# One more slot in seven-product form, and a longer searched order, in a gated MLP kernel

## The chip, the cores and the metric

The kernel runs on one core of a Trainium2 chip. The metric is device time in microseconds (us) of one execution. The core's engines are TensorE (PE; its weight loads are listed as PEld), VectorE (DVE), ScalarE (ACT), GpSimd (POOL) and the sync engine (SP), which issues most DMA transfers. Each engine runs its own row of instructions in order and waits for the others at semaphores.

## What is computed

For each of 4 batches, with 1024 tokens of 512 values:

```
scale = cond @ norm_w.T + 1.0
ms = jnp.mean(x * x, axis=-1, keepdims=True)
h = x * (scale[:, None, :] * jax.lax.rsqrt(ms + EPS))
u = h @ up_w.T                       # up_w: 4096 x 512
val, gate = jnp.split(u, 2, axis=-1)
h = val * jax.nn.gelu(gate, approximate=False)
y = act_quant(h) @ weight_quant(down_w).T
return y + x
```

`act_quant` rounds each token to 8 bits by its largest value, `weight_quant` makes the weights ternary.

## The kernel before

**Work.** The up-projection goes in 16 slots per batch; slot j holds 128 columns of the value and 128 of the gate, for 1024 tokens in two halves. x^T and the weights are split into high and low fp16 parts, and three of the four partial products are summed. A slot comes in one of two forms. The *plain* form (`plain_half`, `plain`, matmul line L1156) takes 12 matmuls of 128x512 for each of value and gate and each half of the tokens, 48 in all. The *seven-product* form (`slot`, `product`, matmul line L1141) treats a slot as 2x2 blocks and makes seven block products of 6 matmuls, 42 in all; it needs sums of weight blocks and sums of x blocks, and more additions behind the matmuls (ACT copies at L1219, L1227 and L1231, gelu at L1236 and L1252; DVE at L1239, L1249, L1255 and L1258, where the plain form has L1180 on ACT and L1184 on DVE). Which slots of the first batch are plain is set by one constant, `SEVEN = 9` (L808): slots 0 to 8 plain, 9 to 15 in seven products. The later batches have seven products throughout. The down-projection (L1362, L1413) is interleaved from the second batch on.

**Weights.** They are loaded once (L774, L777), scaled by a power of two found from their largest value (range L786, L659, L793, L796; scaling L815 on ACT, L817 on POOL), turned (on PE for the first slots, L825 with the copies L850, L852, L853 and L859 to L862; by turning DMA for later ones, L840 to L842), summed (L867 to L870), split (L880, L884) and spilled to DRAM (L888; from slot 9 on, turned first, L895). The later batches load them back: sum parts of slots below `SEVEN` by turning DMA (L909), the others as they are (L911).

**The start.** A condition row is spread over the partitions by a matmul (L685), multiplied with `norm_w` on DVE (L690), shifted (L706), its largest value found (L708, matmul L715, L721), made a power of two (L659, L725), spread again (L731) and inverted (L735, L738). Beside it the sums of squares of the four first blocks of x are taken (L1480 on ACT, L1482 on DVE), POOL makes the reciprocal root (L1001, L1002), the blocks are scaled (L1487 on ACT, L1489 on DVE and POOL), turned on PE (L1494) and split (L1498 on ACT, L1502 on DVE). The first half slot (`plain_first`, L1199) uses them. Warm-up matmuls whose results nobody uses (`keep_warm`, L1510) stand between: 3, 5, 2 and 13 of them.

**Order.** The code does not run in the order in which it is written. Every operation is recorded as a step, with its dependences and an estimated price. `order` places the steps by due time, then goes through a list of seeds: for each one `mend` replays the rows of the engines with randomly changed durations, takes a wait of PE and shifts due times in the chain that led to it. At the end `moved` takes the list `MOVES`: each pair takes one step out of its engine's row and puts it ahead of another. A warm-up matmul has the same price in this model as any other 128x512 matmul.

Of the kernel before, what the change touches and what calls it, by code (L numbers as in the profile page):

```python
# [115 lines left out]
class Plan:  # L116
# [71 lines left out]

    def order(self):

        steps = self.steps
        for s in steps:
            s.after, s.cost, s.soon, s.queue = [], s.alone, 0.0, None
        for s in steps:
            s.pre = [(steps[d], lag(steps[d], s)) for d in s.deps]
            for d in s.deps:
                steps[d].after.append(s)
        clock = 0.0
        self.matmuls = [s for s in steps if s.eng == "PE"]
        for s in self.matmuls:  # L200
            s.start = clock
            clock += s.cost
        chance = random.Random(1)
        self.lucks = [[(chance.random(), chance.random()) for _ in steps] for _ in range(MISSES)]
        for n in range(ROUNDS):
            margin, guard, chained, crowded = MARGINS[n % len(MARGINS)]
            self.needed(clock, chained)
            if crowded:
                self.crowd()
            for s in steps:  # L210
                s.margin, s.guard = margin, guard
            order, kept = self.placed()
            clock = self.replay(order)
        for n in MENDS:
            order, kept = self.mend(order, kept, random.Random(n))
        return self.moved(order)

    def moved(self, order):
# [12 lines left out]
        self.replay([s for row in rows.values() for s in row])  # L231
        return sorted(self.steps, key=lambda s: (s.start, s.n))

    def placed(self):

        kept = [(s.late, s.margin, s.guard, s.soon, s.cost) for s in self.steps]
        self.place()
        return sorted(self.steps, key=lambda s: (s.start, s.n)), kept

    def mend(self, order, kept, chance):  # L240

        steps, last, waits = self.steps, 0.0, []
        for s, k in zip(steps, kept):
            s.late, s.margin, s.guard, s.soon, s.cost = k
        clock = self.replay(order, chance.choice(self.lucks))
        for s in order:
            if s.eng == "PE":
                if s.start - last > 0.08:
                    waits.append((s.start - last, s))
                last = s.end  # L250
        s = chance.choices([s for _, s in waits], [w for w, _ in waits])[0]
        chain, swap, q = [], None, s.behind
        while q is not None and q.eng != "PE" and len(chain) < 20:
            chain.append(q)
            p = q.queue or q.behind
            if p is not None and p.n not in q.deps and chance.random() < 0.5:
                swap = chance.random() < 0.6 and p.eng != "PE" and p.late < q.late
                break
            q = p
        if swap:  # L260
            p.late, q.late = q.late + 2e-3, p.late - 2e-3
        elif chance.random() < 0.3 or not chain:
            t, late = s.start, [s.late for s in steps]
            self.needed(clock, chance.random() < 0.5)
            margin, guard, _, _ = chance.choice(MARGINS)
            for s, old in zip(steps, late):
                if s.tied or not t - 50.0 < s.late < t + 5.0:
                    s.late = old
                    continue
                s.margin, s.guard = margin, guard  # L270
                if s.eng != "PE":
                    s.late -= chance.random() ** 4
        else:
            sooner = 0.2 + 8.0 * chance.random() ** 2
            for q in chain:
                q.late -= sooner
            if chance.random() < 0.2:
                s.late += sooner
        for s in reversed(steps):
            for p in (steps[d] for d in s.deps):  # L280
                if p.eng != "PE" and p.late >= s.late:
                    p.late = s.late - 1e-3
        for s in steps:
            for d in s.deps:
                s.late = max(s.late, steps[d].late + 1e-3)
        return self.placed()
# [65 lines left out]
    def replay(self, order, luck=None):  # L352

        rows = {"PE": [], "ACT": [], "DVE": [], "POOL": [], "SP": []}
        for s in order:
            s.end = -1.0
            rows[s.eng].append(s)
        heads = [[iter(v), None, None, 0.0, None] for v in rows.values()]
        for h in heads:
            h[1] = next(h[0], None)  # L360
        dma, last, port, holder, latest = 0.0, None, 0.0, None, 0.0
        while True:
            first = None
            for h in heads:
                s = h[1]
                if s is None:
                    continue
                if h[2] is None:
                    t, behind = h[3] + s.before, h[4]
                    for d, x in s.pre:  # L370
                        if d.end < 0.0:
                            break
                        x += d.end
                        if x > t:
                            t, behind = x, d
                    else:
                        s.start, s.behind, h[2] = t, behind, t
                if h[2] is not None and (first is None or h[2] < first[2]):
                    first = h
            if first is None:  # L380
                return latest
            s, t = first[1], first[2]
            cost = s.alone
            if luck and s.eng != "PE":
                cost *= 0.96 + 0.12 * luck[s.n][0]
            if s.port:
                if port > t + 0.1:
                    s.behind = holder
                cost += max(0.0, port - t)
                port, holder = t + cost, s  # L390
            s.end = t + cost
            first[1], first[2], first[3], first[4] = next(first[0], None), None, s.end, s
            if s.wait:
                x, s.queue = t + ISSUE, None
                if s.wait > 0.1:
                    if dma > x:
                        x, s.queue = dma, last
                    dma, last = x + s.wait, s
                s.end = x + s.wait + LANDING + (luck[s.n][1] if luck else 0.0)
            if s.end > latest:  # L400
                latest = s.end

# [11 lines left out]
)  # L414
CROWD, ROOM = (45.0, 215.0), 1.05
MOVES = (
# [7 lines left out]
)  # L424
ROUNDS = 1
MENDS = (
# [7 lines left out]
)  # L434
MISSES, ISSUE, LANDING, RELOAD, FETCH, FERRY = 6, 1.2, 1.5, 6.5, 8.6, 4.0


# [113 lines left out]
def glu_quant_kernel(  # L551
# [11 lines left out]
    PE, ACT, DVE, POOL, SP = book.engines(nc)  # L563
# [203 lines left out]
    def wn(j):  # L767
        return H[:, W_SLOT[j]]
# [36 lines left out]

    ROWS = 3

    SEVEN = 9  # L808

    def w_scale(j, ts=(1, 0), eng=None):  # L810
        eng = eng or (ACT if j >= 5 else POOL)
# [22 lines left out]
    def w_rows(j):  # L834
# [3 lines left out]
        f = wn(j).rearrange("p t (n f) -> p (t n) f", n=2)  # L838
        a = 0 if j < SEVEN else 1
        ACT.copy(n[:, a:, 0], f[:, a:])  # L840
# [31 lines left out]
    def s_parts(j):  # L872
        if j >= SEVEN:
            return ((sums_rows, sf),)
# [11 lines left out]
    def s_spill(j):  # L886
# [6 lines left out]
        s = s_tile(j)  # L893
        if j >= SEVEN:
            SP.dma_start_transpose(  # L895
# [1050 lines left out]
    last = NJ // 2 - 1  # L1946
# [159 lines left out]
```

## Time and profile before

| | |
|---|---|
| median of three runs | 719.45 us (719.23 to 719.73) |
| the profiled execution's own time | 719.23 us |
| its span, first to last instruction | 717.4 us |
| busy share of PE, DVE, ACT, POOL | 99%, 84%, 57%, 18% |
| share of PE in the chain that ended last | 97% |

Times in the trace count from the start of the span; 1.8 us of the execution lie around it. In the rows that follow, a line of the timeline gives the start, the busy time, engine, source line, operation, output and inputs, shapes, a count where equal instructions follow each other, and in brackets the idle time before them with what ended it. A grouped line gives busy us and mean ns of one, then idle time ahead of the group.

### The profile page before, as it was taken

The numbers are of one execution on the slowest core, as the hardware profiler recorded it, in microseconds if no ns is written. First come the engines' busy times: TensorE is split into PE (matmuls) and PEld (weight loads), VectorE is DVE, ScalarE is ACT, GpSimd is POOL, SyncE is SP. The second block draws the span as 40 slices with busy tenths as digits, with TensorE's granted clock in tenths as the row PEclk, the third lists the DMA queues.
The fourth block names the chain that finished last, engine by engine and source line by source line (L and its number), as shares of the span: only waits on it lengthen the run. The fifth ranks groups of instructions, "written<-read, shape, count | busy, mean of one in ns | idle before, by whom it ended". The sixth has DMA issues, their size and how long they took to land.

```text
span 717.4 us, 10113 instructions
## 1 busy us (share of the span) xinstructions
PE 711.5 (99%) x3625; PEld 355.8 (50%) x3625; DVE 605.2 (84%) x903; ACT 409.8 (57%) x671; POOL 130.0 (18%) x138
## 2 busy tenths in 40 slices
PE   8999999999999999999999999999999999999998
PEld 4544444444444456664444445665444444445744
DVE  7978998899899899878899887767878888956897
ACT  5677688784546897553435786533333775332454
POOL 4753141020100004660023003700011000000000
PEclk9999999999999999999999999999999999999999
DMA  7778999999785896759234555778233444453414
GB/s 261 253 205 208 240 227 252 194 257 268 219 227 133 210 245 173 223 153 211 67 101 110 118 129 142 176 191 173 73 118 103 102 102 99 99 98 104 150 57 146
DMA packets 189134, 118.74 MB, mean 166 GB/s; under 512 B 151302, under 2 KB 158359, under 8 KB 189084
## 3 DMA queue, kind: packets, MB, share of 16 engines
q1 hardware_dynamic: 188794, 117.77, 64.3%
q8 instruction: 28, 0.46, 0.3%
q10 hardware_dynamic: 290, 0.33, 0.1%
q14 instruction: 22, 0.18, 0.1%
HBM read 59.20 MB, written 23.09 MB: 115 GB/s over the span
## 4 chain that ended last, share of the span: by engine, by line
PE 97%; DMA 1%; ACT 1%; POOL 0%; DVE 0%; issue 0%; SPq 0%; POOLq 0%
PE A L1141 40%; PE E L1141 20%; PE B L1141 10%; PE po L1413 9%; PE E L1156 6%; PE A L1156 4%; PE B L1156 3%; PE po L1362 2%; PE E L1362 1%; PE A L1362 1%; DMA H<-in_x_dram 1%; PE B L1413 1%; PE B L1362 0%; PE A L1199 0%; PE po L1494 0%; PE po L825 0%
## 5 line engine op out<-in xcount | busy, mean ns | idle before, releaser
L1141 PEld LDWEIGHTS <-SXY 128*128 128x128 f16 x2184 | 213.7, 98 | 250.9
L1141 PE MATMUL A<-R,SXY 128*128 128x512 f16 x1188 | 276.3, 379 | 0.0
L1141 PE MATMUL E<-R,SXY 128*128 128x512 f16 x594 | 145.3, 379 | 0.0
L1334 DVE TENSOR_TENSOR H<-H,am 128x1024 f32<-128x1024 f32 x64 | 76.6, 1222 | 0.2
L1141 PE MATMUL B<-R,SXY 128*128 128x512 f16 x312 | 76.6, 379 | 0.0
L1275 DVE TENSOR_REDUCE gm<-H 128x512 f32<-128x1024 f32 x56 | 69.0, 1232 | 0.9
L1252 ACT ACTIVATE t<-t,sg 128x512 f32<-128x512 f32 x55 | 39.7, 721 | 51.0 <-DVE t L1249 51.0
L1239 DVE SCALAR_TENSOR_TENSOR H<-A,sg,t 128x512 f32<-128x512 f32 x55 | 41.2, 749 | 31.9 <-PE A L1141 31.6
L1291 POOL PARTITION_ALL_REDUCE am<-R x8 | 15.5, 1934 | 288.4 <-DVE R L1277 288.4
L1236 ACT ACTIVATE t<-B,sg 128x512 f32<-128x512 f32 x55 | 37.8, 687 | 42.7 <-PE B L1141 42.6
L1227 ACT COPY B<-A 128x512 f32<-128x512 f32 x55 | 31.4, 571 | 53.3 <-PE A L1141 53.1
L1249 DVE TENSOR_TENSOR t<-E,t 128x512 f32<-128x512 f32 x55 | 37.9, 689 | 28.2 <-PE E L1141 27.7
L1413 PE MATMUL po<-wd,R 128*128 128x256 fp8e4 (+1 forms) x448 | 57.0, 275 | 0.0
L1219 ACT COPY t<-A 128x512 f32<-128x512 f32 x55 | 32.2, 585 | 43.4 <-PE A L1141 39.0
L1255 DVE TENSOR_TENSOR v<-A,v 128x512 f32<-128x512 f32 x55 | 37.9, 690 | 20.4 <-PE A L1141 19.6
L1413 PEld LDWEIGHTS <-R 128*128 128x128 bf16 (+1 forms) x480 | 47.0, 98 | 13.1
L1231 ACT COPY v<-E 128x512 f32<-128x512 f32 x55 | 32.2, 586 | 31.9 <-PE E L1141 15.6
L1342 ACT ACTIVATE H<-H 128x1024 f32<-128x1024 f32 x38 | 39.7, 1049 | 8.5 <-DVE H L1334 8.3
L1258 DVE SCALAR_TENSOR_TENSOR H<-v,sg,t 128x512 f32<-128x512 f32 x55 | 41.7, 759 | 1.7 <-ACT t L1252 1.4
L1156 PEld LDWEIGHTS <-SXY 128*128 128x128 f16 x264 | 25.8, 98 | 30.5
L1346 ACT ACTIVATE R<-H 128x1024 bf16<-128x1024 f32 x38 | 39.6, 1052 | 1.0 <-DVE H L1086 0.5
L1277 DVE TENSOR_TENSOR R<-R,gm 128x512 f32<-128x512 f32 x56 | 38.4, 686 | 0.9
(270 smaller groups left out, 919.2 us busy)
## 6 DMA issues: line engine op xcount, KB each, us to landing
SXY<-s_dram SPq DMA_DIRECT2D x57, 256.0 KB, 2.7
H<-in_L_cond_up_w_dram SPq DMA_DIRECT2D x13, 512.0 KB, 4.1
SXY<-s_dram SPq DMA_DIRECT2D x15, 384.0 KB, 3.7
xr<-in_x_dram SPq DMA_DIRECT2D x19, 256.0 KB, 2.9
out_dram<-xr SPq DMA_DIRECT2D x19, 256.0 KB, 2.1
s_dram<-SXY SPq DMA_DIRECT2D x12, 384.0 KB, 3.6
s_dram<-SXY SPq DMA_DIRECT2D x5, 896.0 KB, 6.7
H<-in_x_dram SPq DMA_DIRECT2D x8, 512.0 KB, 4.8
```

The source lines that it names most:

```text
L1141: PE.matmul(o, s[:, w, k, :], xs(l, k), start=start and n == 0, stop=stop and n == len(TERMS) - 1, skip_group_check=True,)
L1156: PE.matmul(ps, a[k // 2][:, w, k % 2, :], XP[:, l, k, h * TOK : (h + 1) * TOK], start=n == 0, stop=n == len(terms) - 1,)
L1239: DVE.scalar_tensor_tensor(h_half(g - 1, 0), prev["A"], gain(g - 1, 0), prev["t1"], ALU.mult, ALU.mult)
L1249: DVE.tensor_tensor(prev["t2"], prev["E"], prev["t2"], ALU.add)
L1252: ACT.activation(prev["t2"], prev["t2"], AF.Gelu, scale=gain(g - 1, 1))
L1258: DVE.scalar_tensor_tensor(h_half(g - 1, 1), prev["v"], gain(g - 1, 0), prev["t2"], ALU.mult, ALU.mult)
L1275: DVE.tensor_reduce(gm[0], v, AX.X, ALU.max, apply_absolute_value=True)
L1277: return [largest, lambda: DVE.tensor_tensor(m, m, gm[0], ALU.max)]
L1334: DVE.tensor_tensor(v, v, r.to_broadcast([P, 2, TOK]), ALU.mult)
L1342: ACT.activation(v, v, AF.Copy, bias=MAGIC)
L1346: ACT.activation(q, by_tile(v), AF.Copy, bias=-MAGIC)
L1413: PE.matmul(po, w[:, j], m, start=start and j == 0, stop=stop and j == n - 1, skip_group_check=True,)
```

## The change

`SEVEN` becomes 8, so that slot 8 of the first batch has the seven-product form and its weights are spilled as those of the slots above it. In the planner the random changes of durations are smaller, `mend` looks for PE's waits only among the first 160, 400, 800 or all PE steps, depending on the seed, and seeds and moves are new lists. The moves, 46 pairs before, are some 330 now; they were searched by a cooled random walk that also kept slightly longer orders. `begin` is called with an empty list and does nothing. Behind the planner every line number is larger by 63.

```diff
@@ def order
+        self.begin(HEAD)
...
-            order, kept = self.mend(order, kept, random.Random(n))
+            order, kept = self.mend(order, kept, random.Random(n), REACH[n % len(REACH)])
@@ def begin (new)
+        if not head:
+            return
...
@@ def mend
-        for s in order:
-            if s.eng == "PE":
-                if s.start - last > 0.08:
-                    waits.append((s.start - last, s))
-                last = s.end
+        for s in [s for s in order if s.eng == "PE"][:reach]:
+            if s.start - last > 0.08:
+                waits.append((s.start - last, s))
+            last = s.end
@@ def replay
-                cost *= 0.96 + 0.12 * luck[s.n][0]
+                cost *= 0.97 + 0.09 * luck[s.n][0]
...
-                s.end = x + s.wait + LANDING + (luck[s.n][1] if luck else 0.0)
+                s.end = x + s.wait + LANDING + (0.7 * luck[s.n][1] if luck else 0.0)
@@ MOVES
-    (1063, 1016), (56, 76), (96, 132), (2119, 2167), (98, 94), (1064, 1016), (307, 275), (295, 31),
...
+    (5604, 5615), (5603, 5614), (5602, 5603), (5598, 5610), (5596, 5597), (5601, 5592), (5607,
...
+REACH = (160, 400, 800, 4000)
+HEAD = ()
...
-    SEVEN = 9
+    SEVEN = 8
```

The order differs on every engine, from the first instructions on. In all, PE has six matmuls fewer: 48 at L1156 go, 42 at the seven-product line come. Three places follow.

On PE, at the start of the program, three warm-up matmuls (the last of them is shown) stand before L685, the spreading of the condition row, and the next follow it:

```order
L1510 LDWEIGHTS H
L1510 MATMUL A_89<-H 128x512
L685 MATMUL B_90<-H,one 128x128
L1510 LDWEIGHTS H
L1510 MATMUL A_91<-H 128x512
```

In the changed kernel ten warm-up matmuls stand before it, of which the last is shown, and L778 (L715 before) is right behind it:

```order
L1573 LDWEIGHTS H
L1573 MATMUL A_91<-H 128x512
L748 MATMUL B_90<-H,one 128x128
L778 MATMUL A_89<-ident,mx_92 1x128
L1573 LDWEIGHTS H
L1573 MATMUL A_89<-H 128x512
```

L748 moved behind seven more warm-up matmuls; before, five of them stood between L685 and L715, now none. Behind L778 come three, then L794 (L731 before), then ten; before it were two and thirteen.

On DVE, at the same place, the row before goes from the products with `norm_w` to the sum of squares of the fourth block of x (L1482) and the range of the first weights (L786):

```order
L690 SCALAR_TENSOR_TENSOR R,scT<-R,B_90 128x128 x4
L706 TENSOR_SCALAR scT<-scT 128x4
L708 TENSOR_REDUCE mx_92<-scT 128x1
L721 TENSOR_REDUCE d_0_93<-A_89 1x1
L722 TENSOR_SCALAR d_0_93<-d_0_93 1x1
L659 TENSOR_SCALAR d_0_93<-d_0_93 1x1
L725 TENSOR_SCALAR dg_94<-ident,d_0_93 1x1
L735 RECIPROCAL ux<-B_90 128x1
L738 COPY dx<-B_90 128x1
L1482 SCALAR_TENSOR_TENSOR R,ssq_0_87<-H 128x512
L786 TENSOR_REDUCE wam_95<-H 128x1
```

The changed row, from L788 (L725 before) on:

```order
L788 TENSOR_SCALAR dg_94<-ident,d_0_93 1x1
L1545 SCALAR_TENSOR_TENSOR R,ssq_0_87<-H 128x512
L849 TENSOR_REDUCE wam_95<-H 128x1
L722 TENSOR_SCALAR wam_95<-wam_95 128x1
L798 RECIPROCAL ux<-B_90 128x1
L856 TENSOR_SCALAR sw<-wam_95 128x1
L801 COPY dx<-B_90 128x1
L859 RECIPROCAL iv_96<-sw 128x1
L1552 TENSOR_SCALAR H<-H,rs_0_88 128x512
```

The seven instructions from L690 to L725 stay ahead of the sum of squares (L1545 now); L798 and L801 (L735 and L738 before) moved behind it.

On ACT, where the split of x^T (L1498) meets the copies of the first slot's turned weights (L852, L853) and the high parts of the first sums (L880), the row before is:

```order
L1498 ACTIVATE R<-po_98,scT 128x512
L1498 ACTIVATE R<-po_97,scT 128x512
L1498 ACTIVATE R<-po_99,scT 128x512
L1498 ACTIVATE R<-A_91,scT 128x512
L880 CAST SXY<-H 128x3x256
L852 CAST SXY<-E_101 128x256
L853 CAST SXY<-E_101 128x256
```

In the changed kernel:

```order
L1561 ACTIVATE R<-po_97,scT 128x512
L1561 ACTIVATE R<-po_98,scT 128x512
L915 CAST SXY<-E_101 128x256
L1561 ACTIVATE R<-po_99,scT 128x512
L916 CAST SXY<-E_101 128x256
L1561 ACTIVATE R<-A_91,scT 128x512
L943 CAST SXY<-H 128x3x256
```

The two copies (L915, L916 now) moved ahead of the last splits and of the cast of the sums.

More of the change, by code (lines that the diff above doesn't have):

```diff
@@ L232, in moved, with begin @@
         return sorted(self.steps, key=lambda s: (s.start, s.n))
+    def begin(self, head):
+        if not head:
+            return
+        first, last, new = set(head), {}, {}
+        self.steps = [self.steps[n] for n in head] + [s for s in self.steps if s.n not in first]
+        for n, s in enumerate(self.steps):
+            new[s.n], s.n = n, n
+        for s in self.steps:
+            s.deps = {new[d] for d in s.deps}
+        for s in self.steps[: len(head)]:
+            if s.wait:
+                continue
+            if s.eng in last:
+                s.deps.add(last[s.eng])
+            last[s.eng], s.tied = s.n, True
     def placed(self):
@@ L238, in placed, with mend @@
         return sorted(self.steps, key=lambda s: (s.start, s.n)), kept
-    def mend(self, order, kept, chance):
+    def mend(self, order, kept, chance, reach):
         steps, last, waits = self.steps, 0.0, []
```

70 rows, old and new, of tables (MENDS, MOVES) are left out of this document.

## The prediction

> **What bounds the kernel now.** I read the profile's first part, then its chain of work that ended last, then a table of busy time by stretch, and last the first 26 us instruction by instruction.
>
> ```profile
> PE 711.5 (99%) x3625; PEld 355.8 (50%) x3625; DVE 605.2 (84%) x903; ACT 409.8 (57%) x671; POOL 130.0 (18%) x138
> PE 97%; DMA 1%; ACT 1%; POOL 0%; DVE 0%; issue 0%; SPq 0%; POOLq 0%
> ```
>
> TensorE (PE) is busy 99% of the span and makes up 97% of the chain: a matmul fewer should shorten the run, and an engine beside it costs something only where PE waits for it. The stretches say where that is:
>
> ```profile
> core 0: us, PE busy (x) PEld busy (x) DVE busy (x) ACT busy (x) POOL busy (x), PEclk, DMA share, GB/s
> 0.00:11.90 11.90, 9.51 (x35) 3.95 (x35) 8.25 (x46) 4.88 (x10) 3.10 (x8) 1.00 0.71 227
> 11.90:24.40 12.50, 12.07 (x71) 7.14 (x71) 11.14 (x24) 8.93 (x20) 10.85 (x14) 1.00 0.91 315
> 24.40:714.40 690.00, 689.92 (x3522) 344.69 (x3520) 585.39 (x834) 395.96 (x642) 116.08 (x117) 1.00 0.64 162
> ```
>
> From 24.4 us on PE never waits: 689.92 of 690.00 us. Before 11.9 us it runs small work and warm-up matmuls, so its busy time there is no measure of use; what the run waits for is another chain, shown below. Time can therefore come from three places: fewer matmuls (A), the start up to the first real matmul (B, and C up to 24.4 us), and stalls that come new in the long middle (D).
>
> **A, six matmuls.** Slot 8 of the first batch has 48 matmuls 128x512 in plain form and 42 in seven-product form; all other slots keep their form. Two steps of the chain, one of each form:
>
> ```profile
> 109.77 2.59 PE E L1156 x12
> 122.72 2.59 PE A L1141 x12
> ```
>
> Both forms run at 2.59 / 12 = 0.216 us a matmul, back to back. Six fewer are 6 x 0.216 = **-1.30 us**, all on the path.
>
> **B, the start.** PE's head, then VectorE's (DVE), then what hangs on them:
>
> ```profile
> 1.26 1.46 PE L1510 MATMUL A<-H 128*128 128x512 f16 x3 [1.26 <-DVE H L607]
> 2.65 0.79 PE L685 MATMUL B<-H,one 1*128 1x128 f32 x2
> 3.37 2.31 PE L1510 MATMUL A<-H 128*128 128x512 f16 x5
> 3.59 0.29 DVE L690 SCALAR_TENSOR_TENSOR R<-R,B 128x128 f32<-128x128 f32 x1
> 5.48 0.42 PE L715 MATMUL A<-ident,mx 128*1 128x128 f32 x1
> 6.60 0.20 DVE L725 TENSOR_SCALAR dg<-ident,d 1x1 f32<-1x1 f32 x1
> 6.86 0.38 PE L731 MATMUL B<-dg,one 1*128 1x1 f32 x2 [0.52 <-DVE dg L725]
> 7.17 2.98 PE L1510 MATMUL A<-H 128*128 128x512 f16 x13
> 7.76 0.69 DVE L1482 SCALAR_TENSOR_TENSOR R<-H 128x512 f32<-128x512 f32 x1 [0.26 <-DMA H<-in_x_dram]
> 8.76 0.19 POOL L1001 TENSOR_SCALAR ssq<-ssq 128x4 f32<-128x4 f32 x1 [8.33 <-ACT R L1480]
> 9.04 1.06 POOL L1002 TENSOR_TENSOR rs<-ssq,neghalf 128x4 f32<-128x4 f32 x1
> 10.14 0.49 DVE L1489 TENSOR_SCALAR H<-H,rs 128x512 f32<-128x512 f32 x1 [0.66 <-POOL rs L1002]
> 10.68 0.55 PE L1494 MATMUL po<-ident,H 128*128 128x128 f32 x3 [0.53 <-DVE H L1489]
> ```
>
> The warm-up matmuls (L1510) are slow at first: five from 3.37 to 5.48 are 0.42 us each. The thirteen from 7.17 take 2.98 us, 0.23 each. So the pace rises at about 5.5 us, 4.2 us after the first of them; the clock column shows 1.00 in both stretches and does not tell them apart.
>
> In the kernel before, three warm-up matmuls stand ahead of L685, which spreads the condition row and starts DVE's chain L690 to L725. In the changed one ten do. DVE's memset for the first of them comes about 0.14 us sooner, so L685 starts at about 1.12 + 10 x 0.427 = 5.4 instead of 2.65: 2.74 later (0.42 by the row of the five; single starts among them are 0.427 apart). DVE's chain follows from it: L690 began 0.94 after L685, L725 ended at 6.80. Shifted by 2.74 that is 9.54; at the fast pace L685 and L715 are shorter by some 0.35 together (0.79 and 0.42 in the slow stretch, about half that afterwards), which gives 9.2. DVE runs its row in order, and in both orders L1482, the sum of squares of the fourth block of x, stands behind L725. It started at 7.76, when the transfer of x had landed; now it starts at 9.2: **+1.4 us**. Everything that it feeds (L1001, L1002, the scaling L1489, the transposes L1494) was waiting for its forerunner, as the brackets show, and the weights' range L786 stands behind L1482 as well, so the shift goes on to PE in full.
>
> Ends: if the pace rises 1 us sooner than in these rows, L685 comes 0.4 to 0.5 sooner (+0.9); if only when DVE's chain is through, +1.8. I take +1.4, the pace rising where the rows show it.
>
> [...]
>
> **C, from 11.9 to 24.4 us.** PE waits at three places there:
>
> ```profile
> 13.04 1.84 ACT L1498 ACTIVATE R<-po,scT 128x512 f16<-128x512 f32 x3 [1.57 <-PE po L1494]
> 14.36 2.10 PE L1199 MATMUL B<-R,SXY 128*128 128x512 f16 x9 [0.37 <-ACT R L1498]
> 15.34 0.85 ACT L880 CAST SXY<-H 128x768 f16<-128x768 f32 x1
> 16.06 0.40 ACT L852 CAST SXY<-E 128x256 f16<-128x256 f32 x1
> 16.51 0.11 PEld L1199 LDWEIGHTS <-SXY 128*128 128x128 f16 x2 [0.55 <-ACT SXY L852]
> 22.13 1.36 POOL L817 TENSOR_SCALAR H<-H,iv 128x512 f32<-128x512 f32 x2 [0.73 <-DVE iv L796]
> 23.23 1.28 PE L825 MATMUL po<-ident,H 128*128 128x128 f32 x8
> ```
>
> First 0.37 for L1498; then 0.2 for L852, which on ScalarE (ACT) stands behind the 0.85 us of L880 (nine matmuls from 14.36 are through at 16.30, the next weights come at 16.51); then small gaps at the turns L825, which wait for POOL's L817. The changed order takes L852 and L853 ahead of L880 and between the L1498s, sets two x transposes ahead of the weight turns, and moves L735 and L738 behind L1482, into DVE's wait for POOL (L1002). A walk through the new rows by these durations gives 0.4 us less up to the first plain half: **-0.4**. Ends: 0 if a transfer is late next (DMA is 0.91 busy in this stretch), -0.55 if all three waits go.
>
> **D, the middle.** The seven-product form costs other engines more:
>
> ```profile
> L1184 DVE SCALAR_TENSOR_TENSOR H<-E,sg,t 128x512 f32<-128x512 f32 x17 | 12.4, 742 | 1.0 <-PE E L1156 0.9
> L1239 DVE SCALAR_TENSOR_TENSOR H<-A,sg,t 128x512 f32<-128x512 f32 x55 | 41.2, 749 | 31.9 <-PE A L1141 31.6
> L1249 DVE TENSOR_TENSOR t<-E,t 128x512 f32<-128x512 f32 x55 | 37.9, 689 | 28.2 <-PE E L1141 27.7
> L1255 DVE TENSOR_TENSOR v<-A,v 128x512 f32<-128x512 f32 x55 | 37.9, 690 | 20.4 <-PE A L1141 19.6
> L1258 DVE SCALAR_TENSOR_TENSOR H<-v,sg,t 128x512 f32<-128x512 f32 x55 | 41.7, 759 | 1.7 <-ACT t L1252 1.4
> 112.00:165.00 53.00, 53.00 (x247) 24.09 (x246) 45.96 (x85) 41.88 (x77) 6.78 (x7) 1.00 1.04 236
> ```
>
> Two L1184 (1.48 us) go, four others (2.89) come: +1.4 on DVE, less 0.3 for a narrower split of that slot's weights (L841). ACT gains three copies in the same way. DVE is idle 7 us of the 53 around the slot, and PE waits for none of it, so the price is nothing while the order keeps slack. By the new DVE row with these means, the tightest place is behind slot 8, some 0.2 us ahead of PE; the tightest in the old one is 0.25 and did not stall. On the sync engine's queue slot 8's weights now make one turning transfer more and are spilled once instead of in three pieces of the same bytes; in each later batch three turning loads become plain ones. DMA is full here (1.04), but these transfers are wanted a batch later. D: **0**, ends 0 and +0.6 (two or three such places missed by 0.2 to 0.3). It cannot give a gain, since PE waits for nothing there.
>
> **Sum.** -1.30 + 1.40 - 0.40 + 0 = -0.3. The profiled execution took 719.23 us (span 717.4 and 1.8 around it), so 718.9; it lies 0.2 below the median of the three runs, 719.45, and from that the forecast is 719.1. With its ends: 718.5 (-1.30 + 0.9 - 0.55 = -0.95) to 720.5 (-1.30 + 1.8 + 0.6 = +1.1).
>
> **Rivals.**
>
> 1. *The head does not lengthen.* If L685 is reached in time, B is nothing: -1.30 - 0.40 = -1.7, **717.75 us**, down to 717.6 with C at its end. That needs the warm-up matmuls fast from the beginning, or L1482 not held by L725. For it: L685's result is needed only for the scale of x^T, at L1498. Against it: the rows at 3.37 and 7.17, and DVE's order.
> 2. *PE falls back to its slow pace.* Between L685 and L731 PE will have only L715 and three warm-up matmuls in about 3 us, where it waited 0.52 at most before. If such a pause of about 2 us ends the fast pace, the ten warm-up matmuls behind L731 take 4.3 us instead of 2.2 and stand in front of the transposes: from 9.5 they end at 13.8 instead of 11.7, and the transposes, due at 10.68 + 1.4 = 12.1, start 1.7 late and are slow themselves, up to 2.3 in all. With 2.0 the sum is +1.7, **721.15 us**, slower. It decides from a pause long enough to lose the pace; no pause of PE over 0.53 us stands in the rows between L685 and L1494, so the trace leaves it open, and does not bear it out.
> 3. *The middle stalls.* The orders differ on every engine throughout. If DVE or a transfer misses PE by a few tenths at several slots, A is given back by +0.6 to +1.3: about **719.9 us**.
>
> [...]
>
> **Chances.** Forecast 0.60; rival 1 0.19; rival 2 0.13; rival 3 0.08. The predicted time is the forecast's, 719.1. The range goes from rival 1's lower end, 717.6, to the upper end of forecast and rival 3, 720.8; rival 2 with 0.13 and some tails are left out. A measurement of this kernel tells about 0.2% (1.44 us) from no change, so faster means below 718.0 and slower above 720.9: faster 0.19 (rival 1), slower 0.13 (rival 2), same 0.68.
>
> **What would show it.** A: 3522 - 6 matmuls behind the head, still without a wait. B: L685 (L748 there) at about 5.4 and L1482 (L1545) at about 9.2 with DVE as its releaser, not a transfer; L1545 at 7.8 would be rival 1. Rival 2: warm-up matmuls behind L731 (L794) 0.42 us apart. C: PE's first wait at L1199 (L1262) no longer for ACT behind L880. D: any wait of PE over 0.1 us after 24 us, above all where slot 9's L1239 (L1302) follows. The forecast fails if the wait for x's transfer, not DVE, sets the start in the changed order, or if C turns into a new wait for the weights.

## The result, and the profile after

| | before | changed |
|---|---|---|
| median, 14 runs each | 719.45 us (718.95 to 721.33) | 721.24 us (720.48 to 721.98) |
| ratio, with its 95% interval | | 1.0024 (1.0016 to 1.0033) |
| the profiled execution's own time, span | 719.23, 717.4 us | 721.98, 720.2 us |

The change made the kernel slower by 0.24%, 1.79 us. The forecast was no change, 719.1 us in a range that ended at 720.8. The changed kernel's profiled execution is the slowest of its fourteen runs, so its trace shows 2.75 us of difference.

It is not the usual execution either. The record gives the mean granted clock of PE for each run. It is 1.000 in the three slowest of the fourteen (721.92 to 721.98 us), 0.995 in two (721.65 and 721.67) and 0.997 or 0.998 in the other nine (720.48 to 721.26). The traces tell what stands behind such a value. In the ninth experiment's profile (same start, 0.998) PE's fast pace (128x512 matmuls 0.216 us apart, 0.427 at the slow one) was reached at 4.4 us, lost at 7.9 and reached again at 11.3; in the second's (0.995) it was lost for 6.8 us. In the trace shown here (1.000) it was reached once, and late, at 13.8 us. A mean of 0.999 comes without such a loss: the profiles of the third, fifth and sixth experiments have it, and read 1.00 in both stretches up to 24.4 us. So by their clocks eleven of the fourteen executions lost the fast pace at the start, and three, as the one traced shows, reached it late.

The first part of the page of the changed kernel, and its table of stretches (columns as in the prediction):

```profile
PE 712.6 (99%) x3619; PEld 356.1 (49%) x3619; DVE 611.9 (85%) x905; ACT 411.5 (57%) x673; POOL 133.8 (19%) x137
```

```profile
0.00:11.90 11.90, 8.58 (x21) 3.14 (x22) 6.66 (x41) 3.86 (x9) 1.70 (x7) 1.00 0.65 201
11.90:24.40 12.50, 12.25 (x67) 7.09 (x66) 9.90 (x23) 8.61 (x19) 10.06 (x13) 1.00 0.84 311
24.40:716.70 692.30, 691.69 (x3533) 345.84 (x3531) 594.84 (x843) 398.98 (x647) 121.99 (x118) 1.00 0.63 162
```

PE executes six matmuls fewer, 3619 against 3625. But from 24.4 us on it has 11 more left than before (3533 against 3522), so it comes to that point later; and it now waits 0.61 us behind it, where it waited 0.08.

The start of the changed kernel, from its timeline (start, busy us, engine, line, operation, in brackets the idle time and its end):

```profile
1.17 4.45 PE L1573 MATMUL A<-H 128*128 128x512 f16 x10 [1.17 <-DVE H L670]
5.55 0.79 PE L748 MATMUL B<-H,one 1*128 1x128 f32 x2
8.12 0.37 PE L778 MATMUL A<-ident,mx 128*1 128x128 f32 x1 [1.78 <-DVE mx L771]
8.87 1.44 PE L1573 MATMUL A<-H 128*128 128x512 f16 x3 [0.37 <-DVE d L784]
9.33 0.67 DVE L1545 SCALAR_TENSOR_TENSOR R<-H 128x512 f32<-128x512 f32 x1
10.23 0.58 PE L794 MATMUL B<-dg,one 1*128 1x1 f32 x2
10.75 3.83 PE L1573 MATMUL A<-H 128*128 128x512 f16 x10
11.59 0.49 DVE L1552 TENSOR_SCALAR H<-H,rs 128x512 f32<-128x512 f32 x1 [0.31 <-POOL rs L1065]
14.41 0.49 PE L1557 MATMUL po<-ident,H 128*128 128x128 f32 x3
```

L748 starts at 5.55 and the sum of squares L1545 at 9.33; the prediction had 5.4 and 9.2. The block that DVE scales is ready at 12.08, 1.45 later than before. But the first transpose does not start then: the ten warm-up matmuls behind L794 take 3.83 us, seven of them at the slow pace, and hold PE until 14.4. The first transpose is 3.73 us later than before (10.68), not 1.4. In the ninth experiment's execution, of the more usual kind, with the same sequence on PE, it is 2.01 later:

```profile
9.82 3.03 PE L1573 MATMUL A<-H 128*128 128x512 f16 x10
12.69 0.49 PE L1557 MATMUL po<-ident,H 128*128 128x128 f32 x3
```

The second new loss is at 151 us. The chain of work between 147 and 153 us, in order of time (start, us, what), then three rows of the timeline there and all cases of the same DVE instruction in the kernel before (L802; min, median and max in ns):

```profile
148.01 0.65 DVE H L1321
148.66 2.01 DVE sg L865
150.67 0.07 DVE iv L859
150.74 0.59 DVE R L1340
151.33 0.61 DVE v L1318
151.98 0.38 PE A L1204
```

```profile
148.45 2.20 POOL L947 TENSOR_TENSOR R<-H,R 128x1024 f16<-128x1024 f32 x1 [16.76 <-ACT R L943]
148.58 2.09 DVE L865 TENSOR_SCALAR sg<-sw,dx 128x2 f32<-128x2 f32 x1
151.98 0.38 PE L1204 MATMUL A<-wd,SXY 128*128 128x512 f16 x1 [0.61 <-DVE v L1318]
```

```profile
L802 DVE TENSOR_SCALAR sg<-sw,dx x16: 208/222/225, 15.8 to 149.4; 128x2 f32<-128x2 f32 x16
```

L865 (L802 before) handles 128x2 values and took between 0.208 and 0.225 us in all 16 cases before. Here it takes 2.09 and ends with POOL's L947 (150.67 and 150.65), which started 0.13 us earlier. PE waits 0.61 us for L1318 at the end of this chain, and by the distance of starts 0.77 us are lost.

The profiled execution by parts: +3.73 first transpose, -1.30 matmuls, +0.77 at 151 us, +0.27 in the last transfer's landing (issued at 717.32 of 720.2, before at 714.87 of 717.4). That is 3.47; the span grew by 2.72. So 0.75 came back between the first transpose and 24 us, where the waits of before (0.37, 0.2 and the small ones) mostly went.

### The profile page after: what moved, and what is told of

The parts are those of the page before. It is cut to its first block, busy times and chain, and to the rows that moved or that the text cites. A ratio compares the mean times of both kernels' runs of the same rounds, so it can differ in the third digit from the quotient of the medians.

```text
span 720.2 us, 10091 instructions
## 1 busy us (share of the span) xinstructions
PE 712.6 (99%) x3619; PEld 356.1 (49%) x3619; DVE 611.9 (85%) x905; ACT 411.5 (57%) x673; POOL 133.8 (19%) x137
## 4 chain that ended last, share of the span: by engine, by line
PE 97%; DVE 2%; ACT 0%; issue 0%
PE A L1204 40%; PE E L1204 20%; PE B L1204 10%; PE po L1476 9%; PE E L1219 5%; PE A L1219 3%; PE B L1219 2%; PE po L1425 2%; PE E L1425 1%; PE A L1573 1%; PE A L1425 1%; PE B L1476 0%; PE B L1425 0%; PE A L1262 0%; PE po L1557 0%; PE B L1262 0%
## 5 line engine op out<-in xcount | busy, mean ns | idle before, releaser
L1397 DVE TENSOR_TENSOR H<-H,am 128x1024 f32<-128x1024 f32 x64 | 79.1, 1261 | 0.1
L1318 DVE TENSOR_TENSOR v<-A,v 128x512 f32<-128x512 f32 x56 | 38.6, 689 | 15.3 <-PE A L1204 14.0
L1321 DVE SCALAR_TENSOR_TENSOR H<-v,sg,t 128x512 f32<-128x512 f32 x56 | 43.0, 769 | 2.0 <-ACT t L1315 1.8
L1340 DVE TENSOR_TENSOR R<-R,gm 128x512 f32<-128x512 f32 x56 | 39.4, 704 | 0.9
```

The lines of the kernel that those rows point to most:

```text
L1321: DVE.scalar_tensor_tensor(h_half(g - 1, 1), prev["v"], gain(g - 1, 0), prev["t2"], ALU.mult, ALU.mult)
L1340: return [largest, lambda: DVE.tensor_tensor(m, m, gm[0], ALU.max)]
L1397: DVE.tensor_tensor(v, v, r.to_broadcast([P, 2, TOK]), ALU.mult)
```

## The experiments

Each is timed beside the kernel before on the same chip, and its difference to that is what is compared. "Changed" stands for +1.79. Moves appended to the list `MOVES` touch only the rows named. The intervals are some 0.65 us to either side (0.9 in the fourth experiment, with five runs), and the difference of two such measurements is less certain still.

**PE's old start in the changed kernel.**

```diff
-(295, 184), (25, 26),
+(295, 184), (25, 26), (35, 34), (48, 58), (49, 58), (58, 61), (59, 61), (60, 61),
```

> The changed kernel with PE's first 26 instructions in the sequence of the kernel before: three warm-up matmuls, the condition row, five, L778, two, L794, thirteen. All other rows as in the changed kernel. Theory 1 (the late condition row and the slow warm-up matmuls in front of the transposes cost the 3.73 us by which the first transpose is late, of which about 0.75 came back up to 24 us): the first transpose at 10.6 to 10.8 us instead of 14.41, the time 721.24 - 3.0 = 718.2, down to 717.5 if what came back stays. Theory 2 (the weights would hold PE in any case, and the loss lies in the new order of the middle): at most 1 us less, 720.3 or more.

Measured 719.49 against 719.59, ratio 0.9998 (0.999 to 1.0007), -0.10: 1.89 less than the changed kernel. From its timeline:

```profile
2.56 0.79 PE L748 MATMUL B<-H,one 1*128 1x128 f32 x2
7.24 2.98 PE L1573 MATMUL A<-H 128*128 128x512 f16 x13
11.16 0.55 PE L1557 MATMUL po<-ident,H 128*128 128x128 f32 x3 [0.93 <-ACT H L1550]
```

The start is the larger part of the loss; theory 2 falls. But the result is 719.5 and not 718.2: the first transpose comes 0.48 later than before, since in the changed row it is that of a block which ACT scales, and two waits up to 16 us stand again (0.15 for L1561, 0.31 for L922). L865 is held here too, for as long as in the changed kernel:

```profile
146.00 2.20 POOL L947 TENSOR_TENSOR R<-H,R 128x1024 f16<-128x1024 f32 x1 [16.77 <-ACT R L943]
146.14 2.09 DVE L865 TENSOR_SCALAR sg<-sw,dx 128x2 f32<-128x2 f32 x1
```

The term that the prediction called C shows no gain when the head is on time.

**Without the ten warm-up matmuls behind L794.**

```diff
-        for s in steps:
+        for s in [s for s in steps if not 60 < s.n < 71]:
```

> The changed kernel without the ten warm-up matmuls behind L794 (nobody uses their results). Theory 1: they held PE from 10.75 to 14.4 us while the transposes' first input was ready at about 12.1; the first transpose comes at 12.1, 2.3 sooner. The transposes then run at the slow pace: up to 1 us of it is lost again. The time 719.2 to 720.2. Theory 2: the same as the changed kernel within 0.4, 721.2.

Measured 721.02 against 719.59, ratio 1.0022 (1.0013 to 1.0031): +1.43, so only 0.4 less than the changed kernel. That is the time of theory 2, but not for its reason: the trace has theory 1's early transposes. Its timeline and a table of stretches cut where the pace changed (PE's busy time is the first column behind the length, PEclk the first behind POOL):

```profile
5.49 0.48 PE L748 MATMUL B<-H,one 1*128 1x128 f32 x2
7.75 0.27 PE L778 MATMUL A<-ident,mx 128*1 128x128 f32 x1 [1.78 <-DVE mx L771]
11.87 0.90 PE L1557 MATMUL po<-ident,H 128*128 128x128 f32 x3 [1.88 <-ACT H L1550]
```

```profile
5.30:8.70 3.40, 1.25 (x6) 0.58 (x6) 2.07 (x13) 2.06 (x6) 0.00 (x0) 1.00 0.77 276
8.70:12.10 3.40, 1.52 (x6) 0.73 (x4) 2.95 (x11) 1.01 (x2) 2.20 (x3) 0.51 0.93 306
12.10:15.50 3.40, 3.40 (x17) 3.40 (x17) 1.47 (x6) 0.68 (x2) 2.87 (x6) 0.50 1.04 384
15.50:17.00 1.50, 1.38 (x10) 0.82 (x9) 1.47 (x4) 1.34 (x4) 1.40 (x2) 0.97 0.98 365
```

The first transpose came at 11.87, 2.5 us sooner, as theory 1 has it. What it got wrong is the price of the slow pace behind it: seventeen transposes at 0.21 instead of 0.11 us take 1.8 of it back, and the first real matmul (L1262) starts at 16.23 instead of 16.93. In this execution the pace had risen by 5.5 us (L748 took 0.48, not 0.79) and was lost at 8.8, after PE had worked 1.25 us in 3.4. It came back at 15.6, after 3.4 us of full work.

**The pause filled.** Five warm-up matmuls are issued again between L748 and L778.

```diff
-        for s in steps:
+        for s in [t for s in steps for t in [s] + [self.steps[n] for n in range(36, 41) if s.n == 35]]:
```

> The changed kernel with five more warm-up matmuls between L748 and L778, in the pause in which PE waited for DVE. Theory 1a (the pace rises after enough unbroken work and the pause undid it): the five run at 0.43 at first, those behind L794 at 0.22 us, the first transpose at about 12.1 instead of 14.41, the time about 719.0 to 719.5. Theory 1b (the pace is slow until a fixed time, pause or not): those behind L794 stay at 0.43, the first transpose at 14.4 or later, the time 721.2 to 721.6.

Measured 720.04 against 719.59, ratio 1.0006 (0.9997 to 1.0015): +0.45, 1.3 less than the changed kernel, with five instructions more, and 0.5 above the time expected by 1a. From its timeline:

```profile
6.27 1.54 PE L1573 MATMUL A<-H 128*128 128x512 f16 x5
9.80 2.33 PE L1573 MATMUL A<-H 128*128 128x512 f16 x10
12.24 0.55 PE L1557 MATMUL po<-ident,H 128*128 128x128 f32 x3
```

The pace rises within the five (1.54 us, where five before took 2.31), and the ten behind L794 take 2.33 instead of 3.83 us; the first transpose comes at 12.24. So 1a holds against 1b: the pause is what kept the ten slow. The record of all runs says the same: the mean granted clock is 0.999 or 1.000 in each of these eleven, so none lost the pace, where eleven of the changed kernel's fourteen did.

**The changed start in the kernel before.**

```diff
-1134), (619, 1038),
+1134), (619, 1038), (35, 47), (48, 35), (49, 35), (58, 54), (59, 54), (60, 54),
```

> The kernel before with PE's first 26 instructions in the sequence of the changed kernel: ten warm-up matmuls, the condition row, L715, three, L731, ten. All else as before. Theory 1: first transpose at about 14.4 instead of 10.68 us, the time 719.45 + 3.0 = 722.4, up to 723.1 if nothing is absorbed. Theory 2: under 720.5.

Measured 722.29 against 719.59, ratio 1.0034 (1.0022 to 1.0047): +2.70. From its timeline:

```profile
10.83 3.83 PE L1510 MATMUL A<-H 128*128 128x512 f16 x10
14.49 0.49 PE L1494 MATMUL po<-ident,H 128*128 128x128 f32 x3
```

The same ten at the same pace, in a kernel whose every other instruction is unchanged. That is more than the 1.89 of the first experiment, but not by more than the intervals allow.

**The held instruction.** The first experiment's moves and, on DVE, L865 ahead of L1321 and L1318 ahead of L1340.

```diff
+(1128, 1268), (1267, 846),
```

> As e1 (PE's old start), and two swaps on DVE near 146 us: L865 ahead of L1321, L1318 ahead of L1340. Theory 3 (L865, a 128x2 instruction that usually takes 0.22 us, took 2.09 because POOL ran L947 at the same time and both wanted the same way to the buffers; PE then waited 0.6 us for L1318): L865 takes 0.2 to 0.3 us again, PE's wait at the seven-product line near 149 us is gone, the time 0.6 to 0.77 less than e1's 719.49, 718.8. Rival (the wait is due to DVE being behind with all its work): L865 is short but PE waits on for L1318 or a later one, the time within 0.2 of 719.5.

Measured 718.60 against 719.61, ratio 0.9982 (0.9974 to 0.9991): -1.01, 0.9 less than the first experiment. DVE and POOL in its timeline:

```profile
144.48 0.22 DVE L865 TENSOR_SCALAR sg<-sw,dx 128x2 f32<-128x2 f32 x1
145.01 2.33 POOL L947 TENSOR_TENSOR R<-H,R 128x1024 f16<-128x1024 f32 x1 [16.76 <-ACT R L943]
146.89 0.69 DVE L1318 TENSOR_TENSOR v<-A,v 128x512 f32<-128x512 f32 x1 [1.47 <-PE A L1204]
```

L865 runs before POOL begins and takes 0.22; DVE now waits 1.47 us for PE where PE had waited for DVE. The rival, a DVE that is behind with all its work, falls. L1318 starts while L947 still runs (to 147.34) and takes 0.69, its usual time, so not every DVE instruction is held. The two swaps were not tried apart. By the changed kernel's trace the first would be enough: it takes 1.87 us off L865, and PE had waited 0.61 for what follows.

**The first transposes in the old sequence**, beside all of the fifth experiment's moves.

```diff
+(85, 90), (86, 90), (87, 90), (88, 90),
```

> As e5, and the four transposes of the block of x that DVE scales (ready first) put ahead of those of the block that ACT scales. If the order of the first turns is what makes the changed start 0.48 us later than before (first transpose 11.16 in e1, 10.68 in the kernel before): first transpose at 10.6 to 10.7 and up to 0.45 less than e5, 718.4. Rival (the last block's turns decide, whichever comes first): within 0.15 of e5.

Measured 718.54 against 719.61, ratio 0.9984 (0.9975 to 0.9992): -1.07, the same as the fifth. The traces do not decide between the two explanations, since the two profiled executions had another pace in front. The row behind L794 of the fifth experiment, then of this one:

```profile
6.82 2.98 PE L1573 MATMUL A<-H 128*128 128x512 f16 x13
```

```profile
7.56 3.84 PE L1573 MATMUL A<-H 128*128 128x512 f16 x13
11.43 0.55 PE L1557 MATMUL po<-ident,H 128*128 128x128 f32 x3
```

PE's sequence up to there is the same in both kernels. The moment at which the pace rises differed between the two executions: the thirteen took 2.98 us in one and 3.84 in the other. The tenth experiment's trace, with the same sequence of transposes as this one and an early rise, has 4.02 us from L794 to the first transpose and 6.80 to the first real matmul, where the fifth's has 4.34 and 6.98. That leaves 0.2 to 0.3 us for the order of the turns, from one execution of each.

**Six matmuls left out of slot 8 in the kernel before.**

```diff
-        for s in steps:
+        for s in [s for s in steps if not 912 <= s.n <= 917]:
```

> The kernel before, with six of the twelve matmuls of one group of slot 8 left out (part of that slot's products is missing). If PE sets the time from 24 us to the end, as the prediction took it for its first term: 719.5 - 1.30 = 718.2. Rival (another engine or a transfer stands close behind PE): less than 0.7 of it, over 718.8.

Measured 718.37 against 719.61, ratio 0.9982 (0.9974 to 0.9991): -1.24 of 1.30. In the stretch from 24.4 us to PE's end it stays busy without a gap, by its table of stretches:

```profile
24.40:713.10 688.70, 688.66 (x3515) 343.92 (x3513) 585.50 (x833) 395.63 (x642) 115.93 (x117) 1.00 0.64 162
```

**No warm-up matmul in the kernel before.**

```diff
-        for s in steps:
+        for s in [s for s in steps if s.n > 70 or s.line != 1510]:
```

> The kernel before without any of its 23 warm-up matmuls. If the pace has to be worked up by PE itself: the 24 transposes run at some 0.21 us each instead of 0.11 and the first plain matmuls at 0.43, 2.5 to 3.5 us more, 722 to 723. Rival (the pace rises by time alone): the same as before within 0.4, 719.5.

Measured 721.08 against 719.61, ratio 1.0021 (1.0012 to 1.003): +1.47, between the two expectations. From its timeline:

```profile
11.37 0.90 PE L1494 MATMUL po<-ident,H 128*128 128x128 f32 x3 [3.85 <-DVE H L1489]
16.54 2.17 PE L1199 MATMUL B<-R,SXY 128*128 128x512 f16 x9
```

The transposes are slow, but the first nine real matmuls run at the fast pace (2.17 us for nine): PE had been at the transposes without a gap from 11.37 to 16.54 us, and that had worked it up. The 23 warm-up matmuls are worth 1.5 us in their old places (0.9 to 2.2 by the interval). In the places that the change gave them they look worse than none: the same kernel took +2.70 with them there (fourth experiment, 1.6 to 3.4), though the condition row is late there as well.

**Only the two swaps on DVE in the changed kernel.**

```diff
+(1128, 1268), (1267, 846),
```

> The changed kernel as it is at the start, with only the two swaps on DVE near 149 us (L865 ahead of L1321, L1318 ahead of L1340). If the head's loss and the held instruction add up independently: 721.24 - 0.85 = 720.4, with the late condition row as the rest. Rival (with the head late, another wait takes the place of this one): within 0.3 of 721.2.

Measured 720.16 against 719.45, ratio 1.0011 (1.0003 to 1.002): +0.71, 1.1 less than the changed kernel. The two losses add up; none takes the other's place.

**Four warm-up matmuls fewer behind L794**, on the sixth experiment's kernel.

```diff
-        for s in steps:
+        for s in [s for s in steps if not 66 < s.n < 71]:
```

> As e6 with nine warm-up matmuls behind L794 instead of thirteen. In e6's profile the pace rose late, the thirteen took 3.84 us, and the first transpose came at 11.43. If late rises are frequent and only the queue costs: 0.2 to 0.5 less than e6, 718.1 to 718.3. Rival (the idle time that the missing four leave lets the pace be lost or rise later, as in the run without the ten): 719 or more.

Measured 718.36 against 719.45, ratio 0.9986 (0.9977 to 0.9995): -1.09, the same as the sixth within what can be told. Its runs spread more widely (717.5 to 720.0 against 717.6 to 719.3), and the clocks in the record part them: seven runs at 1.000 took 717.51 to 718.48, with 717.88 in the middle, and four at 0.997 or 0.998 took 719.08 to 719.99. So both happened, the gain of the shorter row in seven executions and the rival's lost pace in four, and the median hides it. The profiled execution is one of the seven: its PE waited 1.59 us ahead of the first transpose and kept the fast pace. The fifth, sixth and tenth kernels, with slot 8 in seven products and the old start of PE, are the fastest measured, some 1.0 us under the kernel before.

## Why the prediction was wrong

The measured time, 721.24 us, lies above the range, and above the 720.9 from which the prediction called it slower, with a chance of 0.13. By its terms:

| term | forecast | measured |
|---|---|---|
| A, six matmuls | -1.30 | -1.24 (six left out before) |
| B, the start | +1.4 | +1.9 (changed kernel against PE's old start); +2.7 in the kernel before |
| C, 11.9 to 24.4 us | -0.4 | about 0 to +0.25, as the rest of the sum |
| D, the middle | 0 (to +0.6) | +0.9 and +1.1 (two swaps on DVE, twice) |
| sum | -0.3 | +1.79 |

Of the 2.1 us between the forecast's sum and the measured one, D has 0.9 to 1.1, B 0.5 and C 0.4 to 0.65; with the intervals above, the smaller two are rough. The changed kernel without the held instruction (ninth experiment) took 720.16, inside the range. So the start is the larger part of the loss, but most of it was forecast; D is the larger part of the error.

**A** was right: PE sets the time (busy 688.66 of 688.70 us in the seventh experiment's table), and a matmul is 0.216 us.

**B** failed in one step. The row's lateness and DVE's were right to 0.15 us (5.55 and 9.33 for 5.4 and 9.2). The step that failed is "so the shift goes on to PE in full", as if it were all that goes on: the sum has no term for the ten warm-up matmuls behind L794, which at the fast pace would have been through before the transposes' input came (2.33 us for the ten in the third experiment). They ran slowly, all or in part: 3.83 us in the changed kernel's profile, 3.03 in the ninth experiment's.

Rival 2 had named this. It had the fast pace lost in the pause and the first transpose at 13.8 us. In the second and ninth experiments' profiles the pace was lost so (at 8.8 and 7.9 us), and by the listed clocks that is what eleven of the changed kernel's fourteen runs did; the ninth's first transpose came at 12.69. In the changed kernel's profiled execution L748 took 0.79 and L778 0.37 us, so the pace had not risen before the pause, the pause kept it from rising, and the first transpose came at 14.41. In both PE had worked only a part of a stretch of 3.4 us: 1.26 and 1.34 us where the pace was lost, 2.76 and 1.91 where it did not rise. Filling the pause removed it (third experiment). That the rival's time, 721.15 us, is close to the measured one is luck: it has +3.4 for the start, where +1.9 was measured, and nothing for D.

The chance of 0.13 for that was too low. The forecast has no term for a loss of the pace: that a pause of 2 us is harmless was the author's estimate, and no run shows it. The longest single pause in the second experiment's stretch was 1.78 us, and the pace was lost. The last section has what the traces show: how much PE worked in a stretch of 3.4 us.

**C** failed as a size. In the profiled execution 0.75 us did come back there, but because the head was late and so the waits of that stage were over. With PE's old start the new order of that stage shows no gain over the old one: it took away the waits that the prediction names and put others in their place, 0.48 us ahead of the block that ACT scales, 0.15 for L1561 and 0.31 for L922.

**D** was put at 0 and failed on a hold that no part of the prediction named. It compared DVE's work with PE's, found margins of 0.2 us, and bounded a miss by a few tenths. What came was one 128x2 instruction held for 1.9 us beside an instruction on POOL: L865 ends with L947 (150.67 and 150.65), in the first experiment too (148.23 and 148.20), and takes 0.22 us as soon as it runs before it. The common way to the buffers that theory 3 supposes was not shown; the runs show the hold and its end. The kernel before has a case of it, at L659, whose 17 cases have a median of 0.160 us:

```profile
92.22 2.36 POOL L1124 TENSOR_TENSOR H<-H 128x1024 f32<-128x1024 f32 x1 [11.64 <-DVE H L1124]
93.38 1.22 DVE L659 TENSOR_SCALAR wam<-wam 128x2 int32<-128x2 int32 x1
```

They end at 94.58 and 94.60 us, and PE did not wait there. So the place was to be found beforehand in the changed rows of DVE and POOL: a POOL instruction of over 2 us, and behind its start on DVE the small L865 and the rest of a chain that PE needs within 3 us.

Why L947 meets L865 is only partly shown. With PE's old start it met it too (the same 2.09 us), so it belongs to the new order and not to the late head.

## What to carry to other kernels

Put the instruction whose result starts a chain ahead of warm-up work, not behind it, and fill the engine's waits with that work. In the kernel before, where PE worked on until the real work came with no pause over 0.53 us, warm-up matmuls were worth 1.5 us; in the changed one, with a pause of 1.78 us among them, seven of the ten behind it stood in front of the real work at half pace, 0.427 us apart. The planner, which prices them like any other matmul, moved them to the wrong place. When an order is searched, check its long POOL instructions against the small DVE instructions that follow their start on a chain that PE waits for; mean durations show little of it (the twelve L659 up to 112 us in the kernel before have a mean of 0.259 us, with one of 1.22 among them). And compare the profiled execution with the other runs before its trace is taken for the kernel's: here it was of a kind that three runs in fourteen showed.

## What the runs showed of the hardware

The granted clock in the table of stretches reads 1.00 before the pace has risen for the first time (warm-up matmuls up to 4.4 us are 0.43 us apart in every profile here that has them) and 0.5 after it was lost (0.51 and 0.50 from 8.7 to 15.5 us in the second experiment). The trace's record of the clock begins only with the first rise (5.80 us in the kernel before, 13.82 in the changed one), and the table shows 1.00 for what has no record. So a reading of 1.00 at a kernel's start says nothing of the pace; the distance of starts does.

In the two traces with a loss, the changes of the clock lie 3.41 and 3.41 us apart (ninth experiment) and 3.41 and 6.83 (second). Counted in such stretches from each trace's first rise, PE's work in them was:

| profile | stretch, us | PE's work | pace behind it |
|---|---|---|---|
| changed | 3.58 to 6.99 | 2.76 | still slow |
| changed | 6.99 to 10.40 | 1.91 | still slow |
| changed | 10.40 to 13.82 | 3.42 | risen |
| third experiment (pause filled) | 3.47 to 6.88 | 3.41 | risen |
| third experiment | 6.88 to 10.30 | 2.74 | kept |
| ninth | 1.03 to 4.44 | 3.27 | risen |
| ninth | 4.44 to 7.86 | 1.34 | lost |
| ninth | 7.86 to 11.27 | 3.33 | risen |
| second | 5.36 to 8.77 | 1.26 | lost |
| second | 12.18 to 15.60 | 3.42 | risen |
| tenth | 9.12 to 12.53 | 1.82 | kept |
| sixth | 2.52 to 5.93 | 3.30 | still slow |
| sixth | 5.93 to 9.35 | 3.32 | risen |

So the pace rose behind stretches that were nearly full, and not behind 1.91 and 2.76; it was lost behind 1.26 and 1.34 us of work, and kept behind 1.82 and more. The sixth experiment's 3.30 does not fit beside the ninth's 3.27, so the measure is not exact, and where between 1.34 and 1.82 the pace is lost was not tried.

The moment of the rise differed between executions with the same PE sequence: thirteen warm-up matmuls took 2.98 us in the fifth experiment's and 3.84 in the sixth's. The times of kernels with the changed start go with it: in the changed kernel, the fourth and the ninth experiment the runs with a clock of 0.997 or 0.998 are the fastest, those with 0.995 slower and those with 1.000 the slowest (in the changed one 720.48 to 721.26, 721.65 and 721.67, 721.92 to 721.98).
